# A recurrence woven with a mixture of experts: start-up work moved, two sigmoid waits changed, one pacing rule added

## The chip, the core and the metric

The kernel runs on one core of a Trainium2 chip. The metric is the device time of one execution in microseconds, given as the median of several runs; lower is better. The engines are PE (matrix products, with its weight loads shown apart as PEld), DVE (vector), ACT (activations and copies), POOL (general) and SP, which here only issues transfers. Each engine works through its own queue in order and waits for the others by semaphores.

## The reference

Four residual layers follow each other on x, 8 sequences of 512 steps with 256 features, all in 32-bit floats:

```python
x = x + L0(x, cond)   # shared expert silu(x sw1) * (x sw3) @ sw2, plus 2 of 8 routed experts gelu(x rw1) @ rw2
x = x + L1(x, cond)   # a gate per feature: the transform and its inverse cancel, so x times a factor
x = x + L2(x, cond)   # base_down, gelu, base_up, each with a low-rank part made from cond by W2
x = x + L3(x, cond)   # a gated recurrence over the 512 steps, h0 = cond

def step(H, xs):
    xz, xr, xh = xs                       # X @ Wx.T + bx, for each gate
    Z = sigmoid(xz + H @ Whz.T + bhz)
    R = sigmoid(xr + H @ Whr.T + bhr)
    H_tilda = tanh(xh + R * H @ Whh.T + bhh)
    H_new = Z * H + (1.0 - Z) * H_tilda
    Y = H_new @ Whq.T + bhq
    return (H_new, Y)
```

The recurrence has 512 dependent steps; everything before it can be computed ahead of it, window by window.

## The kernel before, in words

Time is cut into 16 windows of 32 steps for all 8 sequences, so a window is 256 columns. `window_jobs` (L497) makes the jobs of a window up to the recurrence's input: products with the shared and routed experts' first weights into a PSUM bank named hp (or low, in window 0), an activation `sig` on ACT, one or two products of it on DVE, for routed experts a product with the routing weight `bc` on POOL, and the products with the second weights into `acc`. Then `lower` (L656) makes layers 1 and 2: `x1` on DVE, `x2` on POOL, products into misc and low with an erf between, and at the end the turned input `xt`, written by POOL (once by ACT). Windows 0 and 1 go through `lower` in two halves. A bank holds two products of 128 x 256, each of two "quads"; a quad (`quads`, L482) is four matmuls of 32 columns of weights, each of which the profile shows as two records, so 8 records.

The order on each engine is not found by the hardware. `Jobs` (L138) is a planner: every job has an engine, the jobs that it depends on, the ring buffers that it uses and a time that it is reckoned to take; `run` (L181) walks a clock of its own and gives each free engine the first job in its queue that is ready, and only then one of a second list, `small`. What it picks is emitted at once, so the program order of each engine is fixed when the kernel is built. Semaphores follow from the tiles: an instruction that writes a bank waits for an earlier one that reads it, also where the two touch different halves.

In the prologue `run` goes on until window 0's last `acc` product and the low-rank weights (`low_in`, made by the products at L1104 from eight 1 MB pieces of W2) are emitted (L1156). Then the code emits outside the planner: the sum of two rows of biases (L1173), twelve clears of the recurrence's buffers (L1185 to L1191) and three bias copies on ACT into the first gates' banks (L1219, called at L1312). Then the planner goes on until the first half of window 0's turned input is emitted (L1314), and for as many PE jobs more as `AHEAD` says, one (L1315). Next come the projections of the first two groups of four steps (L1317, `project` at L1228: per group and half of the features, one piece into the grh bank and one into gz), and the copy of h0 into the state (L1320).

The recurrence's loop (L1362) emits each step: the products of the state for R (`grh<-wh,s_h`), sigmoid, two transposes, the product R * H on DVE (`s_rh`), the products for Z (`gz<-wh,s_h`), the products of `s_rh` for the candidate, tanh, transposes and two scans (L1469) that write the next state. Between them it fills in jobs of later windows: on PE at two places of a step, as many as `first_slot` (L1334, 0 or 1) and `second_slot` (L1342, 1 or 2) say, which compare what is left with a line that falls to nothing at step 462 (`behind`, L1328). From step 3 on a step also emits one of the four pieces of a later group's projection. PE has one queue, so a filler that waits holds what the recurrence has behind it.

Of the kernel before, what the change touches and what calls it, by code (L numbers as in the profile page):

```python
# [9 lines left out]
F32 = mybir.dt.float32  # L10
AF = mybir.ActivationFunctionType
ALU = mybir.AluOpType
# [4 lines left out]
P = 128  # L17
B, T, C = 8, 512, 256
KC = C // P
E = 8  # L20
# [12 lines left out]
FQ = C // NQ  # L33
GS = 4
NG = TC // GS
# [24 lines left out]
TAKES = {"PE": 0.43, "ACT": 0.4, "DVE": 0.4, "POOL": 0.8, "SP": 0.5}  # L60
PE_ALONE, PE_WOVEN = 0.43, 0.65
LEAD = 20
AHEAD = 1
RATE = 0.36
LAG = 3.5

# [137 lines left out]
def cond_resid_kernel(  # L204
# [29 lines left out]
    nc = tc.nc  # L234
# [80 lines left out]
    jobs = Jobs()  # L315
# [161 lines left out]
    for n in range(2):  # L477
        u = const.tile([P, NT], F32, name=f"u{n}")
        nc.vector.memset(u, 0.0)
        us.append(u)  # L480

    def quads(out, lhs, rhs, start, tiles=NQ):  # L482

        for j in range(tiles):
            nc.tensor.matmul(  # L485
                out[ts(j, 32)],
                lhs[:, ts(j, 32)],
                rhs,
                start=start,
                stop=False,  # L490
                skip_group_check=True,
            )
# [4 lines left out]
    def window_jobs(w, routed, xt, via_pool=False):  # L497
# [54 lines left out]
        def bank():  # L552

            turn[0] += 1
            return Lazy(r_low if w == 0 and turn[0] % 3 == 0 else r_h)

        def hidden(lazy, n, lhs, got, first=None):
# [12 lines left out]
                )  # L570
            return made

        later = []

        for m in range(HC):
            h, sig, lin, g = bank(), Lazy(r_sig), Lazy(r_lin), Lazy(r_g)
            j0, j1 = hidden(h, 0, lambda k, m=m: sw13_sb[:, k, 0, ts(m, P)], got_sw13)
            *_, j3 = hidden(
                h, 1, lambda k, m=m: sw13_sb[:, k, 1, ts(m, P)], got_sw13, j0
            )  # L580
            a = add(
                "ACT",
                lambda h=h, sig=sig: nc.scalar.activation(  # L583
                    sig.get(), h.get()[:, 0], AF.Sigmoid
                ),
                [j1],
                [h, sig],
            )
            d = add(
                "DVE",  # L590
                lambda h=h, sig=sig, lin=lin: tt(
                    lin.get(), h.get()[:, 0], sig.get(), ALU.mult
                ),
                [j1, a],
                [h, sig, lin],
            )
            d = add(
                "DVE",
                lambda h=h, lin=lin, g=g: tt(g.get(), h.get()[:, 1], lin.get(), ALU.mult),
                [j3, d],  # L600
                [h, lin, g],
            )
            later.append((g, lambda m=m: sw2_sb[:, m], [d], got_sw2))
            if len(later) > 2:
                into_acc(*later.pop(0))

        for e2 in range(0, E, 2):
            h, j0 = bank(), None
            for n in range(2):
                e = e2 + n  # L610
                got = [got_rw1[e // (E // 2)]] * KC
                j = hidden(h, n, lambda k, e=e: rw1_sb[:, k, e, :], got, j0)
                j0, j = j
                sig, gl, g = Lazy(r_sig), Lazy(r_gl), Lazy(r_g)
                a = add(
                    "ACT",
                    lambda h=h, sig=sig, n=n: nc.scalar.activation(  # L617
                        sig.get(), h.get()[:, n], AF.Erf, scale=RSQRT2
                    ),
                    [j],  # L620
                    [h, sig],
                )
                d = add(
                    "DVE",
                    lambda h=h, sig=sig, gl=gl, n=n: stt(
                        gl.get(), sig.get(), 1.0, h.get()[:, n], ALU.add, ALU.mult
                    ),
                    [j, a],
                    [h, sig, gl],
                    queue=None if w else jobs.small,  # L630
                )
                p = add(
                    "POOL",
                    lambda gl=gl, g=g, e=e: nc.gpsimd.tensor_tensor(  # L634
                        g.get(), gl.get(), bcs[e // 2].get()[:, e % 2], ALU.mult
                    ),
                    [d, fetched[e // 2]],
                    [gl, g, bcs[e // 2]],
                )
# [441 lines left out]
    for n, of in enumerate(LOW):  # L1081
# [59 lines left out]
            0.35,  # L1141
        )

    xts = [Lazy(r_xt) for w in range(NW)]
    l0_ends = []

# [4 lines left out]
    for w in range(2, NW):  # L1151
# [1 line left out]
            ws = list(range(EARLY * (w - 1), EARLY * w))  # L1153
            routes.append(route(ws, late_tiles, r_m, False, ends[w - 1][-1]))
        ends.append(window_jobs(w, routes[w // EARLY], xts[w]))
    jobs.run([l0_ends[0], *got_low_in, *got_small, got_wx, got_wh])  # L1156
    pro.close()


# [8 lines left out]
    with (  # L1168
        tc.tile_pool(name="gw", bufs=1) as gw,
        tc.tile_pool(name="gs", bufs=3) as gs,  # L1170
    ):
        brow = brows[0]
        tt(brow, brow, brows[1], ALU.add)  # L1173


        G_R, G_ZH, G_HH, G_Q = 0, 1, 2, 3
        RH, G_Z = slice(0, 2), 2
        RH_STORED = slice(0, 3, 2)

        s_h, s_rh, d0s = [], [], []
        for u in range(GS):
            s = gw.tile([P, KC, GS, B, 2], F32, name=f"s_h{u}")
            nc.vector.memset(s, 0.0)  # L1185
            s_h.append(s)
            s = gw.tile([P, KC, GS, B], F32, name=f"s_rh{u}")
            nc.vector.memset(s, 0.0)
            s_rh.append(s)
            s = gw.tile([P, KC, B, 2], F32, name=f"d0_{u}")  # L1190
            nc.vector.memset(s, 0.0)  # L1191
            d0s.append(s)

        def across(out, lhs, rhs, start=False):

            return [
                nc.tensor.matmul(  # L1197
                    out[ts(j, 32)],
                    lhs,
                    rhs[:, ..., ts(j, FQ)],  # L1200
                    start=start,
                    stop=False,
                    skip_group_check=True,
                )
                for j in range(NQ)
            ]

        def biases(gates):

            rh, z = gates  # L1210

            def bias(out, row):
                groups = out.shape[1]
                shape = [P, groups, *row.shape[1:]]
                if row.shape[1] == FQ:
                    row = row.rearrange("p (o f) -> p o f", o=1)
                else:
                    row = row.rearrange("p (o g) f -> p o g f", o=1)
                return nc.scalar.copy(out, row.broadcast_to(shape))  # L1219

            half = NG // 2
            return [
                lambda: bias(rh[:, :half], brow[:, RH_STORED]),
                lambda: bias(rh[:, half:], brow[:, RH_STORED]),
                lambda: bias(z, brow[:, 1]),
            ]

        def project(g, gates):  # L1228
# [80 lines left out]
                )  # L1309

        gates = both[0]
        for part in biases(gates):  # L1312
            part()
        jobs.run(ends[0][0])  # L1314
        jobs.run(jobs.queues["PE"][:AHEAD])  # L1315
        base = jobs.now
        for g in range(2):  # L1317
            for part in project(g, gates):
                part()
        nc.vector.tensor_copy(s_h[0][:, :, 0, :, 1], h0)  # L1320
        projected = [Job("PE", None, [], [xts[w]]) for w in range(NW)]
        hists = [
            gw.tile([P, KC, TC, B], F32, name=f"hist_{c}") for c in range(NTC)
# [10 lines left out]
        def first_slot(s, at):  # L1334

            if any(j.done is None for j in ends[1][0]) or jobs.ending() and jobs.left("PE"):
                return 1
            if jobs.left("PE"):
                return 1 if behind(s) and jobs.ready("PE", at + 1.0) > 1 else 0
            return 1 if len(jobs.last["PE"]) > T - s else 0  # L1340

        def second_slot(s, at):  # L1342

            if not jobs.left("PE"):
                return 1
            two = behind(s, 8) or (s + 5) % 2 == 0 and behind(s)
            if two and (any(j.done is None for j in ends[1][0]) or jobs.ending()):
                return 2
            return 2 if two and jobs.ready("PE", at + 1.0) > 2 else 1
# [8 lines left out]
        acts = {  # L1358
            g: [gw.tile([P, FQ], F32, name=f"{g}_{i}") for i in range(2)] for g in "rzc"
        }  # L1360
        upcoming, parts, bias_parts = gates, [], []
        for c in range(NTC):  # L1362
            hist = hists[c]
            gates = upcoming
            for t in range(TC):
# [72 lines left out]
                if 2 * GS <= ahead < T:  # L1438
                    if ahead % GS == 0:
                        assert not parts  # L1440
                        of = upcoming if ahead // TC > c else gates
                        parts = project(ahead // GS, of)
                    part = parts.pop(0)
                    if ahead % WS == WS - 1:
                        projected[ahead // WS].done = now + 1.0
                jobs.fill("PE", now + 0.5, first_slot(s, now + 0.5))
                if part is not None and ahead % 2 == 0:
                    part()
# [6 lines left out]
                cand, act_c = gate(rh[:, n, 1], AF.Tanh, "c", KC)  # L1455
                if part is not None:
                    part()
                jobs.fill("PE", now + 1.44, second_slot(s, now + 1.44))
                if bias_parts and t >= 7:
                    biased.append(bias_parts.pop(0)())  # L1460
# [101 lines left out]
```

## Time and profile before

| What | us |
|---|---|
| Median of 3 runs | 1318.93 (1317.85 to 1319.22) |
| The profiled execution, its own time | 1318.28 |
| Its span, first to last instruction | 1316.5 |
| PE busy | 1178.3 (89%) |
| PE weight loads busy | 688.4 (52%) |
| DVE busy | 916.8 (70%) |
| ACT busy | 505.7 (38%) |
| POOL busy | 150.6 (11%) |
| First scan of the recurrence starts at | 69.4 |
| Last scan starts at | 1310.7 |
| Mean granted TensorE clock | 0.998 |

Busy shares are means over the span. A PE that shows 89% is not a PE at its peak: matmuls overlap, their ends are modelled, and in the recurrence much of its work is filler put where it would otherwise wait. So the table does not say what bounds the time; the waits and the order of the rows do. The transfers lie at the start: of 46.46 MB, 23.07 MB move within the first 80 us.

### The profile page before, as it was taken

What the parts mean: (1) busy time and instruction counts of PE and PEld (TensorE: products, weight loads), DVE (VectorE), ACT (ScalarE), POOL (GpSimd) and SP (SyncE); (2) the same over time, 40 slices, a digit from 0 to 9 for tenths busy, and PEclk for the clock granted to TensorE, in tenths of its full rate; (3) what the DMA queues carried; (4) which work ended last, traced back from release to release, by engine and by line L of the source; (5) the groups of instructions that cost most, each with busy time, mean ns of one, the idle gap of its engine ahead of it and who ended that gap; (6) DMA issues with size and microseconds to landing.
All of it is one profiled execution on the core that took longest, in us unless ns stands there. A gap on an engine that the chain in (4) does not pass through costs nothing.

```text
span 1316.5 us, 88999 instructions
## 1 busy us (share of the span) xinstructions
PE 1178.3 (89%) x39240; PEld 688.4 (52%) x39240; DVE 916.8 (70%) x6271; ACT 505.7 (38%) x3407; POOL 150.6 (11%) x235
## 2 busy tenths in 40 slices
PE   8999999899999999998888988888888888878886
PEld 5666555555555555555554555545554545545443
DVE  5367777777776767676776767677676767667775
ACT  2134343444344444334343433443434344433332
POOL 3311110101011110101011010101101011110000
PEclk9999999999999999999999999999999999999999
DMA  9910001200010010100000010000001000000111
GB/s 318 352 53 16 5 4 38 52 5 29 13 36 20 12 29 5 52 4 28 12 15 26 4 36 4 22 19 12 28 4 29 12 4 4 4 4 4 36 30 26
DMA packets 41859, 46.46 MB, mean 35 GB/s; under 512 B 27488, under 2 KB 31104, under 8 KB 40320
## 3 DMA queue, kind: packets, MB, share of 16 engines
q1 hardware_dynamic: 38576, 38.31, 9.5%
q8 instruction: 306, 5.01, 1.6%
q0 software_dynamic: 1184, 2.31, 0.5%
q14 instruction: 81, 0.66, 0.2%
q10 hardware_dynamic: 1712, 0.16, 0.1%
HBM read 36.45 MB, written 4.33 MB: 31 GB/s over the span
## 4 chain that ended last, share of the span: by engine, by line
PE 66%; DVE 19%; ACT 9%; issue 4%; DMA 2%; SPq 0%; ACTq 0%
PE grh L1197 35%; PE hp L485 11%; DVE d L1393 7%; DVE rT L1393 6%; PE acc L485 6%; PE gz L1197 5%; ACT c L1379 5%; PE low L485 4%; ACT r L1379 4%; PE misc L485 3%; DVE s_h L1469 3%; DVE s_rh L1410 2%; DMA bc<-comb_d 1%; DMA sw_sb<-in_sw_dram 0%; PE misc L1104 0%
## 5 line engine op out<-in xcount | busy, mean ns | idle before, releaser
L1393 DVE STREAM_TRANSPOSE rT<-r 128x32 f32<-128x32 f32 x1024 | 156.1, 191 | 219.5 <-ACT r L1379 215.8
L1379 ACT ACTIVATE r<-grh 128x32 f32<-128x32 f32 x1024 | 146.3, 195 | 421.0 <-PE grh L1197 418.2
L1197 PE MATMUL grh<-wh,s_h 128*32 128x64 f32 x8192 | 221.8, 225 | 90.1 <-DVE s_h L1469 89.1
L1197 PEld LDWEIGHTS grh<-wh,s_h 128*32 128x32 f32 x8192 | 140.4, 109 | 309.6 <-DVE s_h L1469 308.4
L1379 ACT ACTIVATE c<-grh 128x32 f32<-128x32 f32 x1024 | 146.2, 195 | 313.6 <-PE grh L1197 313.1
L1197 PE MATMUL grh<-wh,s_rh 128*32 128x64 f32 x8192 | 221.6, 225 | 34.3 <-DVE s_rh L1410 10.0
L1197 PEld LDWEIGHTS grh<-wh,s_rh 128*32 128x32 f32 x8192 | 139.2, 108 | 191.8 <-DVE s_rh L1410 188.1
L1393 DVE STREAM_TRANSPOSE d<-c 128x32 f32<-128x32 f32 x1024 | 156.5, 192 | 115.2 <-ACT c L1379 108.9
L1197 PE MATMUL gz<-wh,s_h 128*32 128x64 f32 x8192 | 209.9, 219 | 0.4 <-issue 0.3
L1197 PEld LDWEIGHTS gz<-wh,s_h 128*32 128x32 f32 x8192 | 153.5, 110 | 0.9 <-issue 0.8
L485 PE MATMUL acc<-g,rw_sb 128*32 128x256 f32 x2048 | 153.5, 379 | 0.0
L485 PE MATMUL hp<-x,sw_sb 128*32 128x256 f32 x2016 | 150.8, 384 | 2.6 <-ACT sig L583 2.2
L634 POOL TENSOR_TENSOR g<-gl,bc 128x256 f32<-128x256 f32 x128 | 93.6, 733 | 511.9 <-DVE s_h L1469 358.8
L485 PE MATMUL hp<-x,rw_sb 128*32 128x256 f32 x2016 | 151.4, 380 | 0.7 <-ACT sig L617 0.6
L1469 DVE TENSOR_TENSOR_SCAN s_h<-d,d 128x16 f32<-128x16 f32 x1024 | 145.4, 184 | 0.0
L1410 DVE TENSOR_TENSOR s_rh<-rT,s_h 128x8 f32<-128x8 f32 x1024 | 133.5, 168 | 0.0
L1393 DVE STREAM_TRANSPOSE zT<-z 128x64 f32<-128x64 f32 x512 | 121.9, 238 | 0.4 <-ACT z L1379 0.3
L1379 ACT ACTIVATE z<-gz 128x64 f32<-128x64 f32 x512 | 121.4, 237 | 0.8 <-PE gz L1197 0.4
L1483 ACT COPY hist<-s_h 128x16 f32<-128x16 f32 x512 | 106.3, 208 | 0.5 <-DVE s_h L1469 0.5
L1197 PE MATMUL grh<-wx,xt 128*32 128x128 f32 x2048 | 104.8, 274 | 1.3 <-ACT r L1379 1.1
L1422 DVE TENSOR_TENSOR d<-zT,s_h 128x16 f32<-128x16 f32 x512 | 90.7, 177 | 17.5
L1423 DVE TENSOR_SCALAR d<-zT 128x16 f32<-128x16 f32 x512 | 86.8, 169 | 0.0
(154 smaller groups left out, 1208.7 us busy)
## 6 DMA issues: line engine op xcount, KB each, us to landing
bc<-comb_d SPq DMA_DIRECT2D x56, 256.0 KB, 3.2
w<-in_w_dram SPq DMA_DIRECT2D x5, 1024.0 KB, 13.5
out_dram<-x SPq DMA_DIRECT2D x14, 256.0 KB, 3.2
x<-in_w_dram SPq DMA_DIRECT2D x3, 1024.0 KB, 15.6
x<-in_xT_dram SPq DMA_DIRECT2D x2, 1536.0 KB
bc<-comb_d POOLq DMA_DIRECT2D x8, 256.0 KB, 9.0
sw_sb<-in_sw_dram SPq DMA_DIRECT2D x3, 512.0 KB, 8.0
wsq_a<-in_sq_a_dram SPq DMA_DIRECT2D x1, 1280.0 KB
```

The costliest lines, as they stand in the source:

```text
L485: nc.tensor.matmul(out[ts(j, 32)], lhs[:, ts(j, 32)], rhs, start=start, stop=False, skip_group_check=True,)
L634: lambda gl=gl, g=g, e=e: nc.gpsimd.tensor_tensor(g.get(), gl.get(), bcs[e // 2].get()[:, e % 2], ALU.mult),
L1197: nc.tensor.matmul(out[ts(j, 32)], lhs, rhs[:, ..., ts(j, FQ)], start=start, stop=False, skip_group_check=True,)
L1379: nc.scalar.activation(x, y, func)
L1393: ins = nc.vector.transpose(dst.rearrange("p i u b -> p i (u b)"), src.rearrange("p (i r) -> p i r", r=32),)
L1410: prod = tt(s_rh[u][:, k, u, :], rT[:, k, u, :], h[:, k], ALU.mult)
L1422: tt(d1[:, :, u, :, 1], zT[:, :, u, :], h, ALU.mult)
L1423: nc.vector.tensor_scalar(d0[:, :, :, 1], zT[:, :, u, :], -1.0, 1.0, ALU.mult, ALU.add)
L1469: new = nc.vector.tensor_tensor_scan(s_h[v][:, k, v].rearrange("p b w -> p (b w)"), d0[:, k].rearrange("p b w -> p (b w)"), d1[:, k, u].re ...
L1483: nc.scalar.copy(hist[:, :, t, :], s_h[v][:, :, v, :, 1])
```

## The change

It has five parts. The sum of the bias rows, the three bias copies, the clears and the copy of h0 become planner jobs of the list `small`, which may run once the small loads have come and the first half of the low-rank weights is written; the prologue's first `run` ends only when they are emitted. The buffers move to the pool `const`. In window 0 alone, an activation of a bank also depends on the last product into that bank (`j3`, or `ends[1]`), and for the routed experts both products of a bank are made before either activation. `AHEAD` and its `run` go. Only group 0 is projected ahead of the loop; group 1's four pieces are emitted two in step 0 and two in step 1. And `FAR`: while more than 16 products over the line are left, `first_slot` is 1 and `second_slot` 2 without a look at how many are ready.

```diff
-AHEAD = 1
+FAR = 16
...
+    for u in range(GS):
+        s_h.append(const.tile([P, KC, GS, B, 2], F32, name=f"s_h{u}"))
+        s_rh.append(const.tile([P, KC, GS, B], F32, name=f"s_rh{u}"))
+        d0s.append(const.tile([P, KC, B, 2], F32, name=f"d0_{u}"))
+
+    def clear(u):
+        for s in (s_h[u], s_rh[u], d0s[u]):
+            nc.vector.memset(s, 0.0)
+        if u == 0:
+            nc.vector.tensor_copy(s_h[0][:, :, 0, :, 1], h0)
...
@@ window_jobs, shared expert
-                [j1],
+                [j1, None if w else j3],
...
@@ window_jobs, routed experts
-            h, j0 = bank(), None
-            for n in range(2):
+            h, j0, ends = bank(), None, []
+            for e in (e2, e2 + 1):
+                got = [got_rw1[e // (E // 2)]] * KC
+                j0, j = hidden(h, e % 2, lambda k, e=e: rw1_sb[:, k, e, :], got, j0)
+                ends.append(j)
+            for n, j in enumerate(ends):
                 e = e2 + n
-                got = [got_rw1[e // (E // 2)]] * KC
-                j = hidden(h, n, lambda k, e=e: rw1_sb[:, k, e, :], got, j0)
-                j0, j = j
...
-                [j],
+                [j, None if w else ends[1]],
...
+    def small(eng, fn, deps, takes):
+        return jobs.add(eng, fn, deps, (), takes, jobs.small)
+
+    summed = small("DVE", lambda: tt(brow, brow, brows[1], ALU.add), [*got_small, got_low_out[0]], 0.3)
+    got_start = [small("ACT", part, [summed], 0.4) for part in biases(both[0])]
+    got_start += [small("DVE", lambda u=u: clear(u), [summed], 0.4) for u in range(GS)]
...
-    jobs.run([l0_ends[0], *got_low_in, *got_small, got_wx, got_wh])
+    jobs.run([l0_ends[0], *got_low_in, *got_small, got_wx, got_wh, *got_start])
...
-        for part in biases(gates):
+        jobs.run(ends[0][0])
+        base = jobs.now
+        for part in project(0, gates):
             part()
-        jobs.run(ends[0][0])
-        jobs.run(jobs.queues["PE"][:AHEAD])
-        base = jobs.now
-        for g in range(2):
-            for part in project(g, gates):
-                part()
-        nc.vector.tensor_copy(s_h[0][:, :, 0, :, 1], h0)
...
@@ first_slot
+                if behind(s, FAR):
+                    return 1
...
@@ second_slot
+            if behind(s, FAR):
+                return 2
...
-        upcoming, parts, bias_parts = gates, [], []
+        upcoming, parts, bias_parts = gates, project(1, gates), []
...
@@ in the loop, after a piece of a later group's projection is taken, and again behind tanh
+                elif s < 2:
+                    parts.pop(0)()
```

More of the change, by code (lines that the diff above doesn't have):

```diff
@@ L480, in cond_resid_kernel, with biases, bias @@
         us.append(u)
+    s_h, s_rh, d0s = [], [], []
+    for u in range(GS):
[7 more added lines that the diff above has]
+            nc.vector.tensor_copy(s_h[0][:, :, 0, :, 1], h0)
+    brow = brows[0]
+    RH_STORED = slice(0, 3, 2)
+    def biases(gates):
+        rh, z = gates
+        def bias(out, row):
+            groups = out.shape[1]
+            shape = [P, groups, *row.shape[1:]]
+            if row.shape[1] == FQ:
+                row = row.rearrange("p (o f) -> p o f", o=1)
+            else:
+                row = row.rearrange("p (o g) f -> p o g f", o=1)
+            return nc.scalar.copy(out, row.broadcast_to(shape))
+        half = NG // 2
+        return [
+            lambda: bias(rh[:, :half], brow[:, RH_STORED]),
+            lambda: bias(rh[:, half:], brow[:, RH_STORED]),
+            lambda: bias(z, brow[:, 1]),
+        ]
     def quads(out, lhs, rhs, start, tiles=NQ):
@@ L1171, in cond_resid_kernel @@
     ):
-        brow = brows[0]
-        tt(brow, brow, brows[1], ALU.add)
         G_R, G_ZH, G_HH, G_Q = 0, 1, 2, 3
         RH, G_Z = slice(0, 2), 2
[L1178 to L1192, printed above, removed]
         def across(out, lhs, rhs, start=False):
@@ L1205, in across @@
                 for j in range(NQ)
[L1206 to L1225, printed above, removed]
             ]
@@ L1457, in cond_resid_kernel @@
                     part()
+                elif s < 2:
+                    parts.pop(0)()
                 jobs.fill("PE", now + 1.44, second_slot(s, now + 1.44))
```

## The prediction

> **What bounds the kernel now.** I read the page first, then the timeline of PE, ACT and DVE around the start of the recurrence, then sums over stretches, then the waits. The page's chain gives 35% of the span to the recurrence's grh products; the sums show why. Two stretches of equal length, first for the scan line L1469 (two scans a step), then for the filler line L485 (columns: us; busy us of each engine with its count; clock; DMA share; GB/s):
>
> ```profile
> 303.61:381.01 77.40, 9.00 (x64) 1.00 0.06 19
> 1078.63:1156.03 77.40, 9.08 (x64) 1.00 0.02 4
> ...
> 303.61:381.01 77.40, 47.12 (x644) 16.73 (x640) 1.00 0.06 19
> 1078.63:1156.03 77.40, 42.83 (x564) 13.89 (x560) 1.00 0.02 4
> ```
>
> Both hold 64 scans, so 32 steps in 77.40 us or 2.42 us each, with 644 or with 564 filler matmuls. The step is a chain of latencies, and filler fits beside it. The clock is 1.00. The scans run from 69.4 to 1310.7: 511 steps in 1241.3 us, only about 5 over 511 x 2.42 = 1236.6. So what can move is the stretch before step 0's scans (69.4 us), those 5 us, and the 5.6 us after the last step. The change aims at the first.
>
> The chain of waits jumps over this stretch with one piece, a bc transfer of 17.88 us released as ACT r starts. I don't believe it: the r product starts at 67.16 and r at 67.77, 0.61 us later, while one step later the same distance is 70.99 to 71.52, 0.53. So I take the timeline (start, us, engine, line, what, count, idle time before and who ended it). PE:
>
> ```profile
> 16.68 0.64 PE L485 MATMUL low<-x,sw_sb 128*32 128x256 f32 x8 [0.51 <-ACT sig L583]
> 20.90 0.64 PE L485 MATMUL hp<-x,sw_sb 128*32 128x256 f32 x8 [0.57 <-ACT sig L583]
> 24.27 0.64 PE L485 MATMUL hp<-x,rw_sb 128*32 128x256 f32 x8 [0.56 <-ACT sig L617]
> ...
> 57.59 0.64 PE L485 MATMUL hp<-x,sw_sb 128*32 128x256 f32 x8 [1.11 <-ACT sig L583]
> ...
> 66.50 0.43 PE L1197 MATMUL grh<-wx,xt 128*32 128x128 f32 x8
> 66.71 0.32 PE L1197 MATMUL gz<-wx,xt 128*32 128x64 f32 x8
> 66.83 0.43 PE L1197 MATMUL grh<-wx,xt 128*32 128x128 f32 x8
> 67.04 0.32 PE L1197 MATMUL gz<-wx,xt 128*32 128x64 f32 x8
> 67.16 0.43 PE L1197 MATMUL grh<-wh,s_h 128*32 128x64 f32 x16
> ...
> 70.53 0.30 PE L485 MATMUL low<-u,low_out 128*32 128x128 f32 x1 [1.20 <-issue]
> ```
>
> From 10 us on PE has no other idle stretch over 0.3 us before step 0 than these waits for ACT and one of 0.56 at 39.29: PE's own queue is the path. Three waits lie in window 0; the fourth is long because ACT's and DVE's rows read
>
> ```profile
> 56.14 0.78 ACT L1219 COPY grh<-brow 128x256 f32<-128x256 f32 x2 [14.40 <-DVE brow L1173]
> 56.85 0.37 ACT L1219 COPY gz<-brow 128x256 f32<-128x256 f32 x1
> 57.16 0.38 ACT L583 ACTIVATE sig<-hp 128x256 f32<-128x256 f32 x1
> ...
> 55.55 0.55 DVE L1173 TENSOR_TENSOR brow<-brow,brow 128x192 f32<-128x192 f32 x1
> ```
>
> The sigmoid that PE waits for stands behind the three bias copies, and these behind DVE's sum of the bias rows.
>
> **The change, part by part.** Sums are against the profiled execution (1318.28 us, span 1316.5); it lies 0.65 under the median of the three runs, and I carry the difference over to that median.
>
> 1. Clearing and biases amid the prologue. The DVE work is the sum (0.55), twelve memsets (56.08 to 57.13, 1.05) and the copy of h0 (0.17), 1.8 us in all; ACT's is 1.15. They may run once low_out is first written (43.02 on DVE). From there to 53.9 DVE idles 2.52, 2.17 and 3.83 us before its rows, and ACT 14.40: that hides both. If the planner puts a piece ahead of a g product instead, it costs at most one piece, 0.55. No DMA moves. What is gained is the fourth wait: without the biases the sigmoid starts about 56.5, behind the third product (54.98 + 1.50), and PE gets on at 56.95 instead of 57.59. **-0.6** (ends: -0.5, since 0.56 of the 1.11 is the usual wait; -0.64). Late next is the x2 product on POOL, done by 56.4: it has room.
>
> 2. ScalarE behind both products, window 0 only. PE now issues all four quads of a bank and is not held by the activation between the third and the fourth: 0.51 + 0.57 + 0.56 = **-1.64**. The activation starts one quad (0.43) later in its bank; behind it on ACT is nothing urgent (ACT idles 3.13 and 1.22 before such rows), behind it on DVE are lin and g, whose readers come late: g done at 15.81 is read by acc at 18.43. The weight pieces don't stop PE from being earlier: the last, issued at 43.02, moves with PE (the products that free its buffer are earlier too), the four before took 13 to 14 us and were issued by 30.09, and are read from 41.04 on. Ends: 0, if the banks come free 0.43 later and PE waits there instead; -1.64. I take -1.64, since PE has other ready products in each of these places (the router's at 17.13, acc at 21.36 and 24.72). The wait at 39.29 is window 1's and stays.
>
> 3. AHEAD goes, so the low product at 64.82 no longer stands ahead of the projections: the first can start when the turned input is there (POOL 64.38 + 0.41 = 64.79, ACT 64.55 + 0.42 = 64.97) instead of at 65.25. **-0.3** (-0.25 to -0.4). The product takes a slot of step 0.
>
> 4. Group 1's projection leaves the path: 66.50 to 67.16, **-0.66**. Its four pieces come back in steps 0 and 1, beside the recurrence: a grh piece takes 0.21 ahead of the candidate's product, where PE idles 0.22 for s_rh in step 0; a gz piece 0.12 behind it. Steps from 5 on carry the same pieces and three fillers in 2.42. Cost 0 (up to 0.2). The h0 copy at 65.16 was beside the path.
>
> 5. FAR. While the backlog exceeds the target by over 16 products every step asks for 1 + 2 fillers, ready or few. At step 0 the target is 462/482 of what is left; fourteen windows of 72 alone are 1008, so the backlog is 42 and the rule holds from the start. At 3 a step against a target falling by 2.2 it needs at least 33 steps, and longer as output products are added. Until window 1 is through, before does the same anyway; fillers move forward by ten or twenty. Steps don't care (the first fence): 0, ends -0.3 and +0.6, the latter one extra stall of the kind at 70.53.
>
> 6. That stall of 1.20 falls inside one product, 15 of its 16 matmuls issued, with no semaphore behind it. The page has
>
> ```profile
> q8 instruction: 306, 5.01, 1.6%
> ```
>
> 39240 matmuls and as many weight loads are 78480 PE instructions, 256 for each of 306 fetches. I read the stall as PE out of instructions: it follows the densest burst of the run, under a DMA share of 1.05 from 64 to 67, 0.53 to 69.4 and 0.03 after. Here the Trainium skill speaks differently: "Runtime: NRT & Kernel Launch", section "Instruction fetch mechanics", says that the stream is refilled in blocks of 256 instructions and that crossing a block is mostly hidden. By that rule supply costs nothing and the parts above give -3.2. By the row the same block must come while the same transfers run, and the burst now starts about 3 us further into them. If the stall moves along with the instructions it is again 1.2 (cost 0); if the block arrives at the same hour as before, PE starts again at 70.5 and most of the gain is eaten. Ends: -1.3 (gone) and +2.4. I take **+0.2**, close to the row as it stands: the transfers issued behind the last weight piece move forward with PE as well.
>
> Sum: -0.6 - 1.64 - 0.3 - 0.66 + 0.2 = **-3.0**. The profiled execution would be 1315.3; on the median, 1318.93 - 3.0 = **1315.9**.
>
> **Rivals.**
> - *The block of instructions comes at its old hour.* Step 1 then waits at 70.5 as before, having only group 1 and a little more behind it: -0.7, so 1318.2. For it: the DMA share above. Against it: other fetches of the prologue get through a share of 1.0 without a stall over 0.3.
> - *The wait moves instead of going.* The bank's later release holds PE as long as the activation did; part 2 is nothing and the sum -1.4: 1317.5. For it: PE waits on ACT here at all. Against it: DVE's readers have over 2 us in hand.
> - *Forced fillers hold the in-order PE queue (slower).* With FAR the planner sends a product that only just became ready; if on the chip its input is late, PE waits, and the recurrence's products stand behind it. The price is the row's 0.56 each. Ten such waits turn the 3.0 into a loss over 0.2%; at fifteen, 3.0 is turned into +5.4: 1324.3. Against it: from step 0 on PE has no wait for sig in its list at all, though the first steps already fill three a step.
>
> **Chances.** Forecast 0.60, blocks at the old hour 0.12, the wait moves 0.12, forced fillers 0.16. 0.2% is 2.6 us, about what a measurement of this kernel can tell from no change, so "faster" begins below 1316.3, only 0.4 from my forecast. Within the forecast I give faster 0.48 and same 0.12; the first two rivals are within 0.2%, except 0.06 where their parts are partly true and supply is better than I took it. Faster 0.54, same 0.30, slower 0.16. Range: down with every part at its better end (-0.64 - 1.64 - 0.4 - 0.66 - 1.3 - 0.3 = -4.9) to 1314.0; up to the first rival with FAR's 0.6, 1318.8; slower is left out. The forecast's own range is 1314.6 to 1317.2.
>
> **What would show it.** Part 1: L1219's first copies near 44 us, a wait of about 0.56 where 1.11 was. Part 2: no wait for sig in window 0, every later PE row 1.6 us earlier by 50. Part 4: step 0's product straight behind one group of projections, near 64. Part 6: the position and length of the issue stall in steps 0 to 2. Steps still 2.42. The forecast is wrong if step 0 starts later than 65.5, or if steps 1 to 100 lose over 2 us more than now.

## The result, and the profile after

The changed kernel takes **1320.24 us** (median of 22 runs, 1317.06 to 1324.55), the kernel before on the same chip 1318.35 (22 runs, 1316.99 to 1321.57). The ratio is 1.0014, interval 1.0008 to 1.002: slower by about 1.9 us, less than 0.2%. Forecast was 1315.9. The profiled execution took 1319.22, its span is 1317.3 against 1316.5.

The start did what was aimed at, and more. PE's timeline after the change, in the same columns as before (start, us, engine, line, what, count, idle time before and who ended it):

```profile
14.77 1.47 PE L523 MATMUL low<-x,sw_sb 128*32 128x256 f32 x24
...
54.21 0.64 PE L523 MATMUL hp<-x,sw_sb 128*32 128x256 f32 x8 [0.50 <-ACT sig L623]
...
61.78 0.64 PE L523 MATMUL hp<-x,sw_sb 128*32 128x256 f32 x8 [0.51 <-ACT sig L623]
62.24 0.40 PE L1228 MATMUL grh<-wx,xt 128*32 128x128 f32 x8
62.46 0.29 PE L1228 MATMUL gz<-wx,xt 128*32 128x64 f32 x8
62.57 0.40 PE L1228 MATMUL grh<-wx,xt 128*32 128x128 f32 x8
62.79 0.29 PE L1228 MATMUL gz<-wx,xt 128*32 128x64 f32 x8
62.90 0.29 PE L1228 MATMUL grh<-wh,s_h 128*32 128x64 f32 x7
64.62 0.36 PE L1228 MATMUL grh<-wh,s_h 128*32 128x64 f32 x9 [1.44 <-issue]
...
67.61 0.29 PE L1228 MATMUL gz<-wh,s_h 128*32 128x64 f32 x6
69.45 0.33 PE L1228 MATMUL gz<-wh,s_h 128*32 128x64 f32 x9 [1.56 <-issue]
```

The three waits of window 0 are gone, the wait of 1.11 is 0.50, and the recurrence's first product starts at 62.90 where it started at 67.16: **4.26 us earlier**. But seven of its 16 matmuls later PE stands still for 1.44 us, and in step 1 for 1.56, each time inside one product with no semaphore behind it. ACT's timeline has the bias copies where the planner put them, and the sigmoid that they had held up free of them:

```profile
40.97 0.79 ACT L511 COPY grh<-brow 128x256 f32<-128x256 f32 x2 [2.07 <-DVE brow L1189]
41.69 0.37 ACT L511 COPY gz<-brow 128x256 f32<-128x256 f32 x1
53.78 0.38 ACT L623 ACTIVATE sig<-hp 128x256 f32<-128x256 f32 x1 [11.72 <-PE hp L523]
```

The pace of a step is what it was: 64 scans in each of the two stretches of 77.40 us (for the scan line; columns us, busy us of DVE with its count, clock, DMA share, GB/s):

```profile
303.61:381.01 77.40, 9.04 (x64) 1.00 0.07 18
1078.63:1156.03 77.40, 9.10 (x64) 1.00 0.02 4
```

So the gain is lost between steps 0 and 511, and the ends of the steps (their last scans) say where. The excess is the time over 2.418 us a step, the pace of the fences above.

| | before | after | after is ahead by |
|---|---|---|---|
| recurrence's first product starts | 67.10 | 62.84 | 4.26 |
| step 0 ends | 69.73 | 67.40 | 2.33 |
| step 31 ends | 147.40 | 147.25 | 0.15 |
| excess of steps 1 to 31 | 2.72 | 4.90 | |
| excess of steps 32 to 189 | 2.00 | 2.50 | |
| excess of steps 190 to 511 | 0.87 | 1.37 | |
| step 511 ends | 1310.91 | 1311.77 | -0.86 |

(The table takes a modelled start, 0.06 before the timeline's.) 4.26 - 1.93 in step 0 - 2.18 up to step 31 - 0.50 - 0.50 later = -0.85. What PE waited for from 62 to 150 us (us in total, times, longest), before:

```profile
PE low L485 <- issue: 1.2, 1, 1.2
PE grh L1197 <- DVE s_h L1469: 0.6, 2, 0.4
PE gz L1197 <- issue: 0.3, 1, 0.3
PE grh L1197 <- issue: 0.2, 1, 0.2
PE grh L1197 <- DVE s_rh L1410: 0.2, 1, 0.2
```

and after:

```profile
PE gz L1228 <- issue: 2.2, 2, 1.6
PE grh L1228 <- issue: 1.6, 2, 1.4
PE hp L523 <- ACT sig L623: 0.5, 1, 0.5
PE grh L1228 <- ACT r L1390: 0.3, 1, 0.3
PE acc L523 <- issue: 0.2, 1, 0.2
```

"issue" is idle time that no semaphore explains: 1.7 us before, 4.0 after. Most of the new loss is of that kind. The wait for sig ends at 61.78, ahead of the recurrence; the one for ACT's r is new and comes back below.

The trace has a time for every fetch of PE instructions, 306 packets of 16,384 bytes in queue 8, one for each 256 of PE's 78480 instructions. Where such a packet starts (us):

| Block | 5 | 6 | 7 | 8 | 10 | 12 | 14 | 18 | 22 |
|---|---|---|---|---|---|---|---|---|---|
| before | 56.81 | 63.60 | 68.08 | 71.63 | 79.37 | 86.32 | 94.47 | 110.85 | 124.68 |
| after | 55.41 | 62.08 | 66.97 | 70.58 | 77.95 | 85.72 | 95.55 | 110.00 | 124.52 |

PE entered the recurrence 4.26 us earlier, but block 6 came 1.5 us earlier, block 7 1.1, and block 22 0.2. The two kernels issue the same number of PE instructions by the end of step 31, 7439 and 7440, and reach it 0.15 us apart. This says that blocks set the hour, not why they are late.

The places of the stops tie them to the blocks. In order of start, PE goes on after its two long stops with its instructions 1985 and 2241, counted from 0, and both are 193 more than a multiple of 256. The same holds for every stop of 0.3 us or more, from 60 us on, that the timelines of this case put down to "issue", 88 in 18 traces (the two kernels with wide products, below, aside), and each ends 1.2 to 1.6 us after one of these packets has ended. Nor can PE lay up a store: in these traces no packet k, counted from 0, starts before PE stands at 256 k + 180, and PE stops at 256 (k + 1) + 193, so about 270 instructions after a packet can start its block must be there. In starts of instructions, which also show what the modelled ends hide, the stops at these places take 5.7 us from the recurrence's first product to the end of step 31 after the change (those over 0.25 us) and 2.3 before: 3.4 of the 4.1 us lost there.

### The profile page after: what moved, and what is told of

It reads as the page before. It is cut to its first block, busy times and chain, and to the rows that moved or that the text cites. A ratio compares the mean times of both kernels' runs of the same rounds, so it can differ in the third digit from the quotient of the medians.

```text
span 1317.3 us, 89036 instructions
## 1 busy us (share of the span) xinstructions
PE 1177.3 (89%) x39240; PEld 688.4 (52%) x39240; DVE 915.1 (69%) x6271; ACT 507.4 (39%) x3407; POOL 150.5 (11%) x235
## 4 chain that ended last, share of the span: by engine, by line
PE 66%; DVE 19%; ACT 9%; issue 4%; DMA 0%; SPq 0%; ACTq 0%; DVEq 0%
PE grh L1228 35%; PE hp L523 12%; DVE d L1404 7%; DVE rT L1404 6%; PE acc L523 5%; PE gz L1228 5%; PE low L523 5%; ACT c L1390 5%; ACT r L1390 4%; PE misc L523 4%; DVE s_h L1484 3%; DVE s_rh L1421 2%; PE misc L1145 1%; DMA sw_sb<-in_sw_dram 0%; ACT sig L658 0%
## 5 line engine op out<-in xcount | busy, mean ns | idle before, releaser
L523 PE MATMUL hp<-x,rw_sb 128*32 128x256 f32 x2016 | 144.8, 380 | 0.2
```

The source lines that it names most:

```text
L523: nc.tensor.matmul(out[ts(j, 32)], lhs[:, ts(j, 32)], rhs, start=start, stop=False, skip_group_check=True,)
```

## The experiments

Ratios are to the kernel before on the same chip. A profile is of one execution, and where the recurrence starts differs between profiles of kernels that are alike up to there: 65.45 to 68.60 in five of the kernel before and 62.84 to 63.94 in three of the changed one. In some profiles the granted clock also falls to 0.50 for 3.4 us at a time; where that hits a step named below, it is said.

**Can the supply of instructions bound PE at all?** In the kernel before, 32 matmuls of zeros of four columns each were put into every step from 497 on, which then has 256 PE instructions in most steps (about 270 in the first three); or 8 of 256 columns, which add more PE time with fewer instructions. They are issued behind each of a step's two filler places (8 // 2 and 256 in the second kernel) and add zeros to a bank, so no output differs.

```diff
+        def extra():
+            if c == NTC - 1 and t:
+                for n_ in range(32 // 2):
+                    nc.tensor.matmul(other[ts(n_ % NQ, 32), :4], zeros[:, 0:32], zeros[:, :4],
+                                     start=False, stop=False, skip_group_check=True)
...
+                extra()
```

> The kernel before, with 32 extra products of 4 columns (zeros added to a bank that nothing reads again) in each of steps 497 to 511, half of them behind each of PE's two filler places: about 128 PE instructions more a step. Theory A (PE's instructions come in blocks of 256, no two closer than about 3.4 us): 141 + 128 = 269 instructions a step need 3.6 us instead of 2.42, less about 200 that are in stock at the start, so 12 to 16 us over before, with idle stretches of PE that no semaphore ends. Theory B (PE's own working time, or waits of fillers for their inputs): as in supply_few, under 3 us over before.

> The kernel before, with 8 extra products of 256 columns in the same places: the same 0.87 us of PE time a step, but 32 instructions, 173 a step. Theory A: supply reaches 256/3.4 x 2.42 = 182 a step, so no shortage, 0 to 3 us over before for PE's time. Theory B: the same loss as in supply_many.

With many small ones the kernel took 1339.56 us (one execution) against 1320.63, and steps 499 to 511 took 3.07 to 4.79, 3.8 on average; with few wide ones 1320.44 (one execution), and the steps 2.4 to 2.8. In steps 501, 510 and 511 of the first the granted clock was 0.50 for a part of the time; the other ten took 3.6 on average. PE's waits from 1260 us on with the small ones:

```profile
PE grh L1365 <- issue: 10.3, 7, 1.9
PE grh L1197 <- issue: 5.2, 6, 1.6
```

A timeline of PE in two of these steps shows the same form as in the changed kernel, a stop after six matmuls of a product of 16 although their state is long there:

```profile
1297.12 0.31 PE L1197 MATMUL grh<-wh,s_h 128*32 128x64 f32 x6
1298.12 0.36 PE L1197 MATMUL grh<-wh,s_h 128*32 128x64 f32 x9 [0.69 <-issue]
...
1300.49 0.32 PE L1197 MATMUL grh<-wh,s_h 128*32 128x64 f32 x6
1301.59 0.36 PE L1197 MATMUL grh<-wh,s_h 128*32 128x64 f32 x9 [0.79 <-issue]
```

The blocks there are 3.4 to 4.4 us apart, the widest gap beside one of the few transfers of that stretch. So a step of 256 instructions costs a block's spacing: supply is a bound of its own, near 256 / 3.4 = 75 instructions per us or 182 in 2.42 us. A step with three fillers has about 160.

The start of this run's profile shows the change's loss without the change. Up to step 497 it is the kernel before, yet here the recurrence starts at 65.45, 1.65 us earlier than in that kernel's own profile. It stops for 1.47 us in step 1 and ends step 31 at 148.09, 0.69 later.

**Do the transfers delay the blocks?** First the load of x for windows 4 to 15 (two pieces of 1.5 MB, which in the changed kernel still run until 69 us) was held until window 1's turned input was planned.

```diff
-    load_x(NW - EARLY, 1.8)
...
+    load_x(NW - EARLY, 1.8, deps=ends[1][0])
```

> The changed kernel with the 3 MB load of x's later windows held back until window 1's turned input is planned (about step 25), so that it doesn't run while the recurrence starts. Theory A with the limit in the blocks' own spacing: the two stalls of 1.4 and 1.6 us in steps 0 and 1 shrink only by what spacing exceeds 3.4 us there (4.9 once: 1.5 us), and as later blocks stay at 3.4 to 3.6 us the gain is 0 to 1.5 us. Theory C (the blocks are late because of the transfers): both stalls go, 3 us gained, ratio to before 0.999. Theory B: no change, 1.001 to 1.002.

1323.45 us, ratio 1.0024 (1.0015 to 1.0033). Step 0 ends at 66.43 and step 1 has an excess of 0.29 instead of 1.69, so the stalls at the start were that load's. But it now runs from 102.6 to 114.9, and there PE's timeline has

```profile
106.92 0.29 PE L1228 MATMUL gz<-wx,xt 128*32 128x64 f32 x6
110.20 0.22 PE L1228 MATMUL gz<-wx,xt 128*32 128x64 f32 x1 [3.00 <-issue]
```

Blocks 16 and 17 are 7.76 us apart (100.04 and 107.80), and step 17 loses 4.02, a part of it to the clock, which was 0.50 from 111.06 to 114.48. The stall went with the load.

Then the load was cut into three parts, each held until an earlier window was planned; the same with window 1 not in halves and with a group of zero products spread over four steps; and again, with pieces of 128 KB tied to scans.

```diff
+            load_four(w - 2, ends[w - 1][0])
...
-HALVED = 2
+HALVED = 1
...
-                if c == 0 and t == 4:
-                    claim(rh1)
+                if c == 0 and 2 <= t < 6:
+                    claim(rh1, range(2 * t - 4, 2 * t - 2))
...
+            after(made, latest[0])
```

> The changed kernel with the 3 MB load of x's later windows in three parts of four windows, each half MB at a time, held back until windows 1, 2 and 3 are planned. Theory C (transfers delay the blocks): the stalls of steps 0 and 1 go as in x_late, and none of 4 us comes back at step 17, but one of at most 1.5: 2 to 3 us faster than the changed kernel, ratio to before 0.999 to 1.0. Theory A by spacing alone: 0 to 1 us, 1.0005 to 1.0015.

> x_split with window 1 whole, and with the eight products that open the second gate bank spread over steps 2 to 5 instead of all in step 4. If supply and transfers are what the changed kernel lost by, their cures add: step 31 ends 3 to 4 us before the kernel before has it, ratio 0.9965 to 0.998. If not, 1.0 or more.

> The changed kernel with window 1 whole, the second gate bank's opening products spread over steps 2 to 5, and x's later windows loaded in pieces of 128 KB, each tied to the scan of the step before it, so that no more than one runs at a time. If transfers that run for long hold the blocks up, the stall of 2.3 us that the run best has at step 17 goes, and step 31 ends about 3 us before the kernel before has it: ratio 0.9975 to 0.999. If not, as best: 1.0014.

In this order 1.0013 (1.0003 to 1.0024), 1.0014 (1.0006 to 1.0023) and 1.0001 (0.999 to 1.0011). The first two lose 3.09 and 2.26 in step 17, where a part of the load runs; the third loses nothing there, but 1.35 and 0.99 in steps 12 and 13. No order of this load made the kernel faster.

So it was left out of both kernels. Windows 4 to 15 are then made from whatever lies in that buffer.

```diff
-    load_x(NW - EARLY, 1.8)
+    xg.append((EARLY * WS, x_rest))
+    xw.extend(x_rest[:, :, :, ts(i, WS)] for i in range(NW - EARLY))
+    got_x.extend([[None] * KC] * (NW - EARLY))
```

> The changed kernel without the load of x's windows 4 to 15 (their buffer keeps W2's pieces, so windows 4 to 15 are computed from other numbers); everything else is issued as before. Theory C (transfers delay the blocks): the stalls of 1.4 and 1.6 us in steps 0 and 1 go and none comes elsewhere, 2.5 to 4 us faster than the changed kernel, ratio to before 0.998 to 0.9995. Theory A by spacing alone: 0 to 1 us faster, 1.0005 to 1.0015.

> The kernel before with the same load left out (windows 4 to 15 are computed from other numbers). It loses 1.3 us in step 1 and 0.7 in step 4 now; theory C: about 1.3 us faster, ratio 0.999, and no_x_after then 1 to 3 us faster than this one. Theory A by spacing alone: 0 to 0.5 us, and no_x_after is not faster than this one.

Changed 0.9984 (0.9975 to 0.9993), before 0.9985 (0.9977 to 0.9994): both gain, and the change is worth nothing. The changed kernel's step 0 ends at 65.93, 3.6 us ahead of the other's 69.52, and step 31 at 145.83, 0.5 ahead. The largest losses are now in steps 12 and 13:

```profile
93.31 0.61 PE L525 MATMUL acc<-g,rw_sb 128*32 128x256 f32 x6
94.68 0.38 PE L525 MATMUL acc<-g,rw_sb 128*32 128x256 f32 x1 [0.76 <-issue]
...
98.35 0.39 PE L1230 MATMUL grh<-wx,xt 128*32 128x128 f32 x6
99.50 0.27 PE L1230 MATMUL grh<-wx,xt 128*32 128x128 f32 x1 [0.76 <-issue]
```

Three blocks in a row are 5.00, 5.06 and 4.66 us apart there. Across each gap lies one 256 KB load of routing weights (bc): these run from 85.6 to 87.4, 90.5 to 92.5 and 95.6 to 97.3, and the blocks start at 87.37, 92.44 and 97.09.

The last pair leaves those out too: windows 2 to 15 use window 1's routing weights, the planner's jobs and the order on PE stay, and 56 loads of 256 KB are not issued. `Kept` stands in the ring like a buffer of its own and gives window 1's tile.

```diff
         def fetch(i):
+            if w > 1:
+                bcs[i].get()
+                return None
...
+        bcs = [(Lazy if w < 2 else Kept)(r) for r in r_bc]
```

> The changed kernel without the load of x for windows 4 to 15 (as in no_x_after) and without the 56 loads of routing weights (bc, 256 KB each) for windows 2 to 15: these windows use window 1's routing weights, so their output is made from other numbers. Theory A, a transfer that runs holds back the next block of 256 PE instructions until it ends: the gaps of 5.0, 5.1 and 4.7 us between blocks near 82, 87 and 92 us in no_x_after, each of which spans one such load, fall to 3.4 to 3.6; the stalls of steps 9 to 13 (2.8 us together) are gone; step 31 ends near 143 instead of 145.8, which is at least 1.5 us ahead of no_bc_before; time about 1315 to 1316.5, ratio about 0.996. Theory B, blocks have their own rhythm in this part of the run whatever moves: block 22 stays within 1 us of 123.1, step 31 within 1 us of 145.8, and there is no lead over no_bc_before.

> The kernel before with the same loads left out. Theory A: the gaps of 4.0 to 5.2 us between blocks near 84, 89 and 94 us in no_x_before fall to 3.4 to 3.6, its stalls at steps 11 and 13 (0.9 us together) are gone, step 31 ends near 145.3; time about 1317 to 1318, ratio about 0.998. Theory B: step 31 stays within 0.5 us of 146.4.

Changed 1313.55 us, 0.9949 (0.9935 to 0.9963); before 1314.33, 0.9952 (0.9939 to 0.9964). The blocks of the changed kernel near 82, 86, 90 and 93 us are 3.41, 4.05 and 3.41 apart, and step 31 ends at 142.54, 3.3 us earlier than with the loads. The kernel before ends it at 145.06. **The changed kernel's lead at step 31 is 2.52 us, not 0.15.** PE's waits of the changed kernel over the whole recurrence now hold one entry for supply:

```profile
PE grh L1248 <- DVE s_h L1504: 88.7, 301, 0.8
PE grh L1248 <- DVE s_rh L1441: 8.6, 20, 0.6
PE grh L1248 <- ACT r L1410: 1.9, 10, 0.3
PE hp L538 <- ACT hist L1518: 1.0, 1, 1.0
PE hp L538 <- ACT sig L643: 0.5, 1, 0.5
PE gz L1248 <- issue: 0.2, 1, 0.2
```

The first product that stopped at seven matmuls runs through:

```profile
62.72 0.41 PE L1248 MATMUL grh<-wh,s_h 128*32 128x64 f32 x16
62.94 0.41 PE L1248 MATMUL gz<-wh,s_h 128*32 128x64 f32 x16
```

That blocks keep their own hours whatever moves is thereby refuted. Not all of the lead stays: 4.04 at the start, 2.52 at step 31, 1.43 at the end, and the medians (of 5 executions each) are 0.78 apart, with intervals of the ratio that overlap. So a shorter time of the whole changed kernel is not shown even here; what is shown is where the lead went.

The 1.5 us lost up to step 31 have two main causes. Group 1's pieces cost about 0.5: step 0 takes 0.27 longer than in the kernel before without these loads and step 1 0.21, because the first piece writes the bank that ACT's r still reads, and PE, in order, waits with the filler and the product behind it:

```profile
63.66 0.43 PE L1248 MATMUL grh<-wx,xt 128*32 128x128 f32 x8 [0.31 <-ACT r L1410]
63.90 0.62 PE L538 MATMUL low<-x,wsq_a 128*32 128x128 f32 x16
64.33 0.41 PE L1248 MATMUL grh<-wh,s_rh 128*32 128x64 f32 x16
```

That product starts 1.61 us behind the step's first one, and 1.37 in the kernel before. Most of the rest is supply again, without a large load: in steps 24, 25 and 28 PE pauses for 0.30, 0.44 and 0.37 us from start to start, again at 193 past a block's edge, and modelled ends hide most of that from the wait list; the kernel before without these loads has none over 0.25 up to step 31.

**Fewer instructions instead of fewer transfers.** Window 1 whole instead of in halves takes 225 PE instructions out up to step 31 in the changed kernel and 257 in the kernel before; or the changed kernel takes one filler less in steps 0 to 3 (in `second_slot`).

```diff
-HALVED = 2
+HALVED = 1
...
...
+            if s < 4:
+                return 1
```

> The changed kernel with window 1 not halved (HALVED = 1): its layers 1 and 2 take 256 PE instructions less in the first 27 steps, for the same arithmetic. Theory A: one block less in the stretch where blocks are the limit, so 2 to 3.4 us faster than the changed kernel: 1316.8 to 1318.2 where that has 1320.2, ratio to before 0.999 to 1.0. Theory B (forced fillers, FAR): as many fillers are forced, no gain, ratio 1.001 to 1.002.

> The kernel before with window 1 not halved: one block of PE instructions less in steps 0 to 25. Theory A: of its 2.7 us of loss in steps 1 to 31 about half goes, ratio 0.999 to 0.9998. If the loss there is not supply, 1.0.

> The changed kernel with at most two fillers in steps 0 to 3 in place of three: the burst is thinner, but window 1 must still be through by step 27, so the number of PE instructions by then is the same. Theory A in the form 'the sum of the first 25 steps counts': the stalls in steps 0 to 4 get shorter, later ones longer, step 31 ends within 0.5 us of the changed kernel's, ratio to before 1.0005 to 1.002. In the form 'the burst counts': 1.5 to 3 us faster than the changed kernel, ratio 0.999 to 1.0.

1.0000 (0.9992 to 1.0009), 0.9993 (0.9985 to 1.0002) and 1.0000 (0.9991 to 1.0008). In the first, step 31 ends at 145.80, 1.45 earlier than in the changed kernel, but 1.37 and 1.19 are lost in steps 47 and 56. The loss of step 47 is not supply: the granted clock was 0.50 from 181.06 to 184.47. That of step 56 is a stop of 0.74 beside a load of 1 MB. In the third, step 0 still ends at 68.33 and step 17 loses 1.13. None of the three is faster than the kernel before.

Then the four matmuls of 32 columns that make a quad became one of 128 columns, a quarter of the instructions:

```diff
-        for j in range(tiles):
+        wide = P if tiles == NQ else 32
+        for j in range(32 * tiles // wide):
...
-                out[ts(j, 32)],
-                lhs[:, ts(j, 32)],
+                out[ts(j, wide)],
+                lhs[:, ts(j, wide)],
```

> The kernel before, with each quad (four products of 32 columns of weights) issued as one product of 128 columns: a quarter of the fillers' PE instructions, the same arithmetic; the recurrence's own products stay as they are. Theory A (supply of PE instructions) says the shortages of the start go: about 4 of the 5.6 us that its steps lose over 2.42 us come back, ratio 0.997, unless a product of 128 columns holds PE longer than a quad's 0.43 us, which no row of the trace shows; then it is slower, by as much as it takes more. Theory B (forced fillers, late inputs): no gain, 1.0 or more.

> The changed kernel with the same edit. Theory A: with supply out of the way the 4.3 us by which its recurrence starts earlier stay, so 3 to 4.5 us faster than wide_before, whatever that one takes. Theory B: still about 2 us slower than wide_before, as the changed kernel is to the one before.

1423.4 and 1423.88 us, ratios 1.0774 (1.0756 to 1.0793) and 1.0783 (1.0766 to 1.08). The stall of step 1 in the kernel before fell from 1.33 to 0.23, but PE itself became the bound. Its sum from 303.61 to 381.01, with the wide products and then in the kernel before:

```profile
303.61:381.01 77.40, 75.43 (x1787) 1.00 0.05 17
```

```profile
303.61:381.01 77.40, 71.24 (x2436) 1.00 0.06 19
```

97% of the stretch, with fewer steps done in it. So this pair can't show what the lead would be worth: it took away the supply limit and put another in its place.

**The parts of the change.** The kernel before with the parts of the start (biases, clears, group 1, no AHEAD), without the later sigmoid and FAR; with FAR alone; with the later sigmoid and FAR. In the first the constant is so large that its rule never holds; the other two have 16.

```diff
-AHEAD = 1
+FAR = 100000
...
+                if behind(s, FAR):
+                    return 1
...
-                [j1],
+                [j1, None if w else j3],
```

> The kernel before with the start-up parts alone: clearing and biases amid the prologue, no AHEAD, group 1's projection in steps 0 and 1; not the waits on both products of a bank and not FAR. Theory A: step 0's products start about 2 us earlier and what they gain is given back in steps 0 to 25, ratio 0.9995 to 1.001. Theory B (FAR's fillers are the loss): the gain stays, 0.998 to 0.999.

> The kernel before with FAR alone. Theory A: steps 0 to 25 are as they were (three fillers a step already), later steps are a little denser and lose 0 to 1 us where blocks are late, ratio 1.0 to 1.0008. Theory B: the whole loss, 1.001 to 1.003.

> The kernel before with the waits on both products of a bank in window 0, and FAR, without which window 2's input is not planned in time. Theory A (supply of PE instructions): step 0 starts about 2 us earlier, and steps 0 to 25 give it back, ratio 0.9995 to 1.001, with step 31 ending within 0.7 us of where it ends with FAR alone. Theory B (the loss comes from the start-up parts): ratio 0.998 to 0.9995.

1.0001 (0.9992 to 1.0011), 1.0005 (0.9996 to 1.0013), 1.0002 (0.9993 to 1.001): none differs from the kernel before. The first starts the recurrence at 65.66 and then loses 2.9 and 1.21 us in steps 1 and 2; the stop in step 1 is 2.26, and from 72.53 to 75.94, in parts of both steps, the granted clock was 0.50. The third starts it at 66.20. The later sigmoid without FAR, and the full change without FAR, were not tried, so FAR's share in the loss of the full change stays open.

None of the kernels with the full work beats the kernel before. The nearest, the kernel before with window 1 whole, is at 0.9993 with 1 inside its interval.

## Why the prediction failed

The direction was wrong, and the failure is in the main in one term.

- **Part 1** (0.6): right. The copies stand at 40.97 on ACT, the wait of 1.11 is now the usual 0.50.
- **Part 2** (1.64): right in kind, too small in size. No wait for sig is left in window 0 and no bank's wait took its place, so the rival that the wait moves is out. PE's rows near 50 us are 2.8 earlier where this part promised 1.64. From start to start the three waits cost 2.28, not 1.64, since the profile's idle time begins only at the modelled end of the last matmul (from the start of the 24 at 14.77 to the next product it is now 1.29 us; for the same 24, with the wait among them, it was 2.01). Most of the rest comes from the first 15 us, where PE reached its full pace earlier in this profile (8 records from 12.51 to 13.04; before, 8 from 12.12 to 12.98).
- **Part 3** (0.3): hardly anything. A window 1 product that waits for sig (61.78) again stands ahead of the projections, which start 0.21 after the turned input (62.03) where it was 0.28.
- **Part 4** (0.66): the gain was larger and the cost was not 0. From the first projection to the first product it was 1.91 us and is 0.66; about 0.5 of that gain was a stop for instructions (1985, at 66.17), which has only moved behind the first product. The four pieces cost about 0.5 in steps 0 and 1, since the working left out that a piece waits for r. So 4.26 us at the start, against 3.2 for all four parts, is more than was won.
- **Part 5** (0): alone, FAR is within the interval of no change. From step 0 on there is no wait for sig: forced fillers that wait for data, the slower rival, are not what happened.
- **Part 6, the failed step.** "I take **+0.2**, close to the row as it stands", with +2.4 as the far end. From the recurrence's start on, 4.26 + 0.85 = **5.1 us** were lost: 1.93 in step 0, 2.18 in steps 1 to 31, 1.0 after. Up to step 31, stops for instructions longer than before account for 3.4 of them and group 1's pieces for about 0.5. I had priced supply as one stall with one position, although the page's 306 fetches of 256 instructions give a rate that PE runs close to. The first rival, a block that comes at its old hour, had the mechanism, but it was given a chance of 0.12 and a price that kept 0.7 us of the gain, because I applied it to one block. In the changed kernel blocks 5 to 22 of the table come at most 1.5 us earlier than before, and block 14 comes 1.1 later.

My reason against that rival was that other fetches of the prologue get through a DMA share of 1.0 without a stall over 0.3. That was no evidence: the prologue is slower in instructions (its blocks are 7 to 11 us apart), with wider products, and a late block is noticed only by an engine that is close behind it. The rule of the Trainium skill that I weighed ("Runtime: NRT & Kernel Launch", section "Instruction fetch mechanics": crossing a block is mostly hidden) is nearly true of the changed kernel without the loads, where the wait list of the whole recurrence has 0.2 us of such waits, and not of the kernel with them, nor of steps with 256 instructions; the measurement decides.

Shown by the runs: supply can bound PE; the stops of the start are waits for blocks; a transfer in flight can hold back the next block; without the large load and the routing loads the lead at step 31 is 2.5 us instead of 0.15, in one profile of each. Open: what makes a block late beside a transfer (a place in a queue or a shared engine), and where 1.1 us of the lead go after step 31 without these loads, in losses of at most 0.26 a step. Step 4 loses 0.5 to 0.6 in both kernels without loads too; there stands the group of zero products, and where it is spread over steps 2 to 5 these lose 0.2 to 0.3 each instead. The changed kernel is slower than the one before by 1.9 us in the medians and by 0.85 in the two profiles; the losses above were read from the profiles.

## What to carry to other kernels

When PE runs many small matmuls, count its instructions per microsecond against the spacing of its instruction fetches (here 256 in about 3.4 us at best; no two blocks of the traces start less than 3.2 apart) before you price an earlier start: work that starts sooner than its instructions come gains nothing. Idle time inside a product with no semaphore behind it is the sign, its place in PE's count of instructions is the test (here always 193 past a block's edge), and the transfers in flight at that moment are the first suspects, even those of 256 KB that look harmless by their share. Price such a stall as a rate over the whole stretch in which the engine runs close to its supply, not as one event. Look also at the granted clock of a step before you explain its loss, and read a wait's cost from start to start.

## What the runs showed of the hardware

A 256 KB load of routing weights stretched the gap between two instruction blocks from 3.4 to 3.6 us to 4.7 to 5.1, and 3 MB of x stretched one to 7.76; taking 56 such small loads and the large one away made either kernel about 0.5% faster, more than the whole change had promised. PE's stops for instructions all end at the same place of a block, 193 instructions past its edge. And a filler quad as one matmul of 128 columns is not cheaper than four of 32: it left PE 97% busy and the kernel 7.7% slower, although it has a quarter of the instructions.
